# A state-space layer stage: one of four B products moved to GpSimd, six scan tiles, B single-buffered, dt spread one group earlier

## The chip, the cores and the metric

The kernel runs on one core of a Trainium2 chip. The metric is the device time of one launch in microseconds (us), median of several runs; lower is better. The core has five engines with queues of their own: TensorE (PE: matrix products into PSUM), VectorE (DVE), ScalarE (ACT: activations and copies), GpSimd (POOL) and SyncE (SP, here the queue from which most DMAs are issued).

## The reference, cut to what matters

The reference is four blocks in a row on an image of 2 x 128 x 64 x 64; the change touches the first alone. That block runs two layers over a sequence of 4096 positions with 128 channels. A layer is a selective state-space mixer followed by a feed-forward block:

```
t2 = layernorm(t);  xz = t2 @ in_w.T;  u, z = split(xz)
u = silu(causal_conv4(u) + conv_b)                      # 256 channels
dt, Bm, Cm = split(u @ xproj_w.T, [8, 24])              # 8 | 16 | 16
dt = softplus(dt @ dt_w.T + dt_b)                       # 256 channels
dA  = exp(dt[..., None] * A);  dBu = (dt * u)[..., None] * Bm
h   = dA_t * h + dBu_t          # for each of 256 x 16 states, along the sequence
y   = sum_n h[n] * C_t[n] + u * D;  t = t + (y * silu(z)) @ out_w.T
t   = t + gelu(layernorm(t) @ w1.T + b1) @ w2.T + b2
```

The other three blocks (a convolutional attention, a linear-projection attention and a multi-scale fusion) follow; their code is not touched.

## The kernel before, in words

All arithmetic is float32. The first block is written by hand as one long order of instructions (`tc.manual_schedule()`): nothing is reordered, each engine executes its own instructions in the order in which Python emits them, and waits between engines are put in from the tiles that they read and write.

The work is cut into 32 **items** (image b, layer l, chunk c of 512 positions; `items`). The scan of an item needs 256 x 16 states = 4096 rows of 512 positions; with 128 partitions this is 32 scan instructions. They form 8 **groups** g of 4: a group covers 32 channels, partition 32q+d holds channel d with state 4q+m, and m = 0..3 are the four scans of the group. So an item has 32 **slots** t, one scan each, and group g has slots 4g to 4g+3. (In this text the groups of an item are numbered 0 to 7, and the first groups of the next item continue as n0, n1.)

For one group these helpers run, always in this order of data:

- `spread_dt` (L329): four DMAs on SP copy 32 channels of dt to all four partition quarters, tile `dtb` (four buffers). Emitted at the first slot of a group for the group two ahead.
- `decay` (L347, ACT): `da` = exp(A * dtb), one per scan, emitted four slots ahead of its scan, into one of four PSUM buffers. So `da` for slot t+4 needs the buffer of scan t.
- `spread_dtu` (L334, PE): dt*u spread to the quarters by a matrix product, tile `pdu`, one PSUM buffer, emitted one group ahead. It has to wait until the product of the group before has read `pdu`.
- `times_b` (L340, DVE): the **B product** `h` = `bb` * `pdu`, 128 x 2048 (all four m at once), emitted in the last slot of the group before. `bb` holds B of the item, spread to 128 partitions by DMA (two buffers).
- `scan` (L358, DVE): four scans, each 128 x 512, in place in `h`. After the fourth GpSimd saves the last column (L360, `carry`) and multiplies by C (L361, `h` = `h` * `cb`, 128 x 2048).
- `y_pair` (L373, PE): sums over the states of two groups, every second group; `y_out` (L381, DVE) adds u * D when half an item is complete.

`h` tiles come from a ring of five, tag `h`, which also serves the feed-forward's `hid`.

Around this the function `background` emits, slot by slot, the rest of the layer for neighbouring items: for the next item (n) the convolution (slots 0 to 5, L262, L268), silu (slot 11, L282), the x projection (13, 14, L291, L295), softplus of dt (17, L315), dt*u on GpSimd (18, L321); for the item before (p) the second `y_out` and the gate on GpSimd (6, L381, L384), the mixer's output product and its add (8 and 10, L390, L394), the feed-forward's upper half (30, 31, L403); for the one before that (q) gelu and the lower half (3 to 9, L407, L415, L424). Two layer norms share one chain: variance (17, L210 on PE), epsilon and reciprocal root on ACT (18, 19, L214 to L221), and one Newton step: a product on GpSimd, an affine step on ACT, a product on GpSimd (20 and 21, L226, L227, L231), spread on PE and scaled on DVE (27, 28, L235, L239).

The places in the order that matter here, inside one slot: first the spreads, then the scan, then the decay of slot t+4, then (last slot of a group) the B product of the next group, then the background of that slot. B and C are sent through DRAM (`spread_bc`): one store and eight spreading DMAs, 256 KB each, all at slot 14 on SP, ahead of the dt spreads of later groups in the same queue.

```
if m == 0 and 0 <= g + 2 < NG:
    spread_dt(g + 2)
...
if m == 3 and 0 <= g + 1 < NG:
    times_b(g + 1)
for f, a in todo[t_]:
    f(*a)
```

Of the kernel before, what the change touches and what calls it, by code (L numbers as in the profile page):

```python
# [6 lines left out]
F32 = mybir.dt.float32  # L7
AF = mybir.ActivationFunctionType
ALU = mybir.AluOpType
# [6 lines left out]
P = 128  # L16
CH = 512
# [3 lines left out]
DS = 16  # L21
DI = 2 * C
NJ = DI // P
R = (C + 15) // 16
NX = R + 2 * DS
KC = 4
# [41 lines left out]
def tile_conv_seq(ctx: ExitStack, tc, x, consts, vecs, wemb, wlay, wconv, wdt, wqkv, wsmall, wms, out):  # L68
    nc = tc.nc
# [38 lines left out]
    with ExitStack() as s, tc.manual_schedule():  # L108
# [25 lines left out]
        for l in range(NL):  # L134
            w = wp.tile([P, NWL - DI], F32, name=f"wl{l}")
            nc.sync.dma_start(w, wlay[l][:, DI:])
            cw = sp.tile([P, KC + 1, DI], F32, name="cw", tag="h", bufs=5)
            nc.sync.dma_start(cw[:, :KC, :].rearrange("p k d -> p (k d)"), wconv[l : l + 1, :].to_broadcast([P, KC * DI]))
            nc.sync.dma_start(cw[:, KC, :], wlay[l][:, :DI])
            d = wp.tile([R, DI], F32, name=f"wd{l}")  # L140
            nc.sync.dma_start(d, wdt[l])

            u = wp.tile([P, KC, DI], F32, name=f"wu{l}")
            for k in range(KC):
                nc.vector.tensor_tensor(u[:, k, :], cw[:, KC, :], cw[:, k, :], ALU.mult)
            an = wp.tile([P, NJ * DS], F32, name=f"an{l}")
            nc.scalar.activation(an, vec[:, VEC[f"A_log{l}"] : VEC[f"A_log{l}"] + NJ * DS], AF.Exp)
            nc.vector.tensor_scalar(an, an, -1.0, None, ALU.mult)
            a = wp.tile([P, NJ, 4, 4], F32, name=f"am{l}")
            for g in range(4):  # L150
                pa = mm.tile([P, NJ, DS], F32, name="pa", tag="mm")
                nc.tensor.matmul(pa.rearrange("p j n -> p (j n)"), lhsT=four(g), rhs=an, start=True, stop=True)
                for q in range(4):
                    at = slice(32 * q, 32 * q + 32)
                    nc.vector.tensor_copy(a[at, :, g, :], pa[at, :, 4 * q : 4 * q + 4])
            wl.append(w), wu.append(u), wd.append(d), am.append(a)
# [40 lines left out]

        def ln_square(w, k, i):
            if "sq" not in w:
                w["sq"] = sp.tile([P, 2, CH], F32, name="sq", tag="tmp", bufs=2)  # L200
                w["cen"] = sp.tile([P, 2, CH], F32, name="cen", tag="cen")
            pc = w.pop(("pc", k))
            nc.scalar.activation(w["sq"][:, k, :], pc, AF.Square)
            nc.scalar.copy(w["cen"][:, k, :], pc)
# [35 lines left out]

        def ln_shift(w, k, i, second):
            if second:
                dst = st[i]["x2"] = sp.tile([P, CH], F32, name="x2", tag="tmp", bufs=2)
            else:
                xn = st[i]["xn"] = sp.tile([P, KC - 1 + CH], F32, name="xn", tag="xn", bufs=2)
                if items[i][2] == 0:
                    nc.gpsimd.memset(xn[:, : KC - 1], 0.0)
                else:
                    nc.gpsimd.tensor_copy(xn[:, : KC - 1], prev_xn[0][:, CH : CH + KC - 1])
                prev_xn[0] = xn  # L250
                dst = xn[:, KC - 1 :]
            nc.scalar.activation(dst, w["cen"][:, k, :], AF.Identity, bias=vl("ln_b", i))  # L252
# [41 lines left out]
            st[i]["dbl"] = sp.tile([NX, CH], F32, name="dbl", tag="dbl")  # L294
            nc.scalar.copy(st[i]["dbl"], st[i].pop("pd"))  # L295

        def spread_bc(i):

            dr = dp.tile([2 * DS, CH], F32, name="dr", tag="dr")
            nc.sync.dma_start(dr, st[i]["dbl"][R:])  # L300
            for k in range(2):
                o = st[i]["bc", k] = sp.tile([P, 4, CH], F32, name=("bb", "cb")[k], tag=("bb", "cb")[k], bufs=2)
                for q in range(4):
                    src = dr[k * DS + 4 * q : k * DS + 4 * q + 4, :].rearrange("(o m) f -> o (m f)", o=1)
                    nc.sync.dma_start(o[32 * q : 32 * q + 32].rearrange("p m f -> p (m f)"), src.to_broadcast([32, 4 * CH]))

        def dtproj(i, j):
            st[i]["pt", j] = mmt("pt")
# [15 lines left out]
        def spread_dt(g):  # L324
            i, s_ = divmod(g, NST)
            o = st[i]["dtb", s_] = sp.tile([P, CH], F32, name="dtb", tag="dtb", bufs=4)
            k = 32 * (s_ % 4)
            for q in range(4):
                nc.sync.dma_start(o[32 * q : 32 * q + 32, :], st[i]["dt"][k : k + 32, s_ // 4, :])  # L329

        def spread_dtu(g):
            i, s_ = divmod(g, NST)
            pdu = st[i]["pdu", s_] = bc.tile([P, CH], F32, name="pdu", tag="bc")
            nc.tensor.matmul(pdu, lhsT=four(s_ % 4), rhs=st[i]["dtu"][:, s_ // 4, :], start=True, stop=True)  # L334

        def times_b(g):
            i, s_ = divmod(g, NST)
            h = st[i]["h", s_] = sp.tile([P, 4, CH], F32, name="h", tag="h", bufs=5)
            pdu = st[i].pop(("pdu", s_))
            nc.vector.tensor_tensor(h, st[i]["bc", 0], pdu.unsqueeze(1).to_broadcast([P, 4, CH]), ALU.mult)  # L340

        def decay(t):
            g, m = divmod(t, 4)
# [53 lines left out]
        def ffn_up(i, f):  # L397
            w = st[i]
            if f == 0:
                w["hid"] = sp.tile([P, 4, CH], F32, name="hid", tag="h", bufs=5)  # L400
            ph = mmt("ph")
            at = WL_W1 + f * P
            nc.tensor.matmul(ph, lhsT=wl[items[i][1]][:, at : at + P], rhs=w["x2"], start=True, stop=True)  # L403
            nc.scalar.activation(w["hid"][:, f, :], ph, AF.Identity, bias=vl("ffn_b1", i, f))
# [32 lines left out]
        def background(i):  # L437

            todo = [[] for _ in range(NSL)]

            def at(t, f, *a):
                todo[t].append((f, a))

            n, p, q, r = i + 1, i - 1, i - 2, i + 2
            if has(q):
                at(3, gelu, q)
                at(6, ffn_down, q, (0, 1)), at(7, ffn_down, q, (2, 3)), at(9, ffn_add, q)
                at(11, out_mm, q), at(12, out_add, q)
            if has(p):
                at(6, y_out, p, 1), at(6, gate, p)  # L450
                at(8, mix_out, p), at(10, mix_add, p)
            if has(n):
                at(0, pu_taps, n, 0, (0, 1)), at(1, pu_taps, n, 0, (2, 3)), at(2, pu_out, n, 0)
                at(3, pu_taps, n, 1, (0, 1)), at(4, pu_taps, n, 1, (2, 3)), at(5, pu_out, n, 1)
                at(13, xproj, n), at(14, xproj_out, n), at(14, spread_bc, n)
                at(15, dtproj, n, 0), at(16, dtproj, n, 1), at(17, soft_plus, n), at(18, dt_end, n)
            if has(i):
                at(1, pz_mm, i, 0), at(3, pz_out, i, 0)
                at(5, pz_mm, i, 1), at(6, pz_out, i, 1)
            if has(i) or has(n):  # L460
                at(11, silu, i, n)
            pair = [(k, second) for k, second in ((p, True), (r, False)) if has(k)]
            if has(r):
                at(10, embed, r), at(11, embed_out, r)
            w, m = {}, len(pair)
            for k, (it, second) in enumerate(pair):
                at(12 + 2 * k, ln_centre, w, k, it)
                at(13 + 2 * k, ln_square, w, k, it)
                at(27, ln_spread, w, k, m), at(28, ln_scale, w, k, it)
                at(29, ln_shift, w, k, it, second)  # L470
            if pair:
                at(17, ln_var, w, m), at(18, ln_eps, w, m), at(19, ln_rs, w, m), at(20, ln_newton, w, m), at(21, ln_step, w, m)
            if has(p):
                for f in range(4):
                    at(30 + f // 2, ffn_up, p, f)
            if has(i):
                at(23, y_out, i, 0)
            return todo
# [6 lines left out]
        for i in range(-2, NI + 2):  # L485
            todo = background(i)
            for t_ in range(NSL):
                t = i * NSL + t_
                g, m = divmod(t, 4)
                if m == 0 and 0 <= g + 2 < NG:  # L490
                    spread_dt(g + 2)
                if m == 0 and 0 <= g + 1 < NG:
                    spread_dtu(g + 1)
                if m == 0 and g % 2 == 1 and 0 <= g - 3 < NG:
                    y_pair(g - 3)
                if 0 <= t < NT:
                    scan(t)
                if 0 <= t + 4 < NT:
                    decay(t + 4)
                if m == 3 and 0 <= g + 1 < NG:  # L500
                    times_b(g + 1)
                for f, a in todo[t_]:
                    f(*a)


    wbig = ctx.enter_context(tc.tile_pool(name="wbig", bufs=1))
# [11 lines left out]
    with ExitStack() as s, tc.manual_schedule():  # L518
# [10 lines left out]
        st = {}  # L529
# [151 lines left out]
        def at(f, u0):  # L681

            r, u = divmod(now - u0, NU)
            if 0 <= r < len(runs):
                f(r, u)
# [485 lines left out]
```

## Time and profile before

Median 5351.36 us (5349.31 to 5352.06). The profiled execution has a span of 5360.6 us. The stage of the first block runs from the start to about 2170 us of it; its steady part, read as a window from 80 to 2170 us of the span:

| engine | busy us in 2090 us | share | what it mostly does there (mean of one) |
|---|---|---|---|
| DVE | 1882.7 | 90% | 1024 scans (1267 ns), 256 B products (2266 ns) |
| PE | 1835.1 | 88% | state sums, spreads, convolution, projections |
| ACT | 1472.6 | 70% | 1024 decays (685 ns), six table loads an item (1283 ns) |
| POOL | 1430.7 | 68% | 256 C products (4534 ns), dt*u, gate, two norm products an item |

The mean granted TensorE clock in the window is 0.89. How to read what follows: "busy" is the sum of the durations of an engine's instructions; an instruction's "idle before" is the time in which its engine stood still just ahead of it, put down to what ended last. The timeline lists instructions of one engine in order of time, equal ones in a row merged ("x3"), with that idle time in brackets.

### The profile page before, as it was taken

What the parts mean: (1) busy time and instruction counts of PE and PEld (TensorE: products, weight loads), DVE (VectorE), ACT (ScalarE), POOL (GpSimd) and SP (SyncE); (2) the same over time, 40 slices, a digit from 0 to 9 for tenths busy, and PEclk for the clock granted to TensorE, in tenths of its full rate; (3) what the DMA queues carried; (4) which work ended last, traced back from release to release, by engine and by line L of the source; (5) the groups of instructions that cost most, each with busy time, mean ns of one, the idle gap of its engine ahead of it and who ended that gap; (6) DMA issues with size and microseconds to landing.
All of it is one profiled execution on the core that took longest, in us unless ns stands there. A gap on an engine that the chain in (4) does not pass through costs nothing.

```text
span 5360.6 us, 48695 instructions
## 1 busy us (share of the span) xinstructions
PE 4900.6 (91%) x15085; PEld 2311.3 (43%) x15085; DVE 3798.2 (71%) x3810; ACT 2326.4 (43%) x2933; POOL 2287.5 (43%) x1948
## 2 busy tenths in 40 slices
PE   5888888888888898899999999999999998988997
PEld 1222222222222222356665566656666665333332
DVE  4998999889999999136663366667767775656665
ACT  4676777777777776212221122232323221223332
POOL 2766666666666767112221122223333332322221
PEclk8898889999898988899999999999999999999998
DMA  4222233222222232014442244444444442000000
GB/s 108 69 65 64 65 70 70 68 68 64 64 64 64 68 73 69 17 42 95 96 97 50 51 96 96 95 101 112 112 101 101 112 111 71 4 4 4 6 6 8
DMA packets 233843, 362.04 MB, mean 68 GB/s; under 512 B 87648, under 2 KB 88048, under 8 KB 225136
## 3 DMA queue, kind: packets, MB, share of 16 engines
q1 hardware_dynamic: 184432, 291.76, 23.2%
q10 hardware_dynamic: 49152, 67.17, 5.2%
q8 instruction: 121, 1.98, 0.2%
q14 instruction: 138, 1.13, 0.1%
HBM read 83.92 MB, written 6.29 MB: 17 GB/s over the span
## 4 chain that ended last, share of the span: by engine, by line
PE 59%; DVE 14%; DMA 10%; ACT 6%; SPq 4%; issue 4%; POOL 4%; ACTq 0%; DVEq 0%; POOLq 0%
PE pq L600 11%; PE po L647 11%; PE py L373 5%; PE pp L544 5%; DVE tr L627 4%; PE pu L262 4%; SPq L638 3%; DMA dtb<-dt 3%; DVE h L358 3%; DMA bb<-dr 3%; POOL h L361 3%; DMA pt<-tr 3%; PE pdu L334 2%; PE pf L861 2%; PE ph L403 2%
## 5 line engine op out<-in xcount | busy, mean ns | idle before, releaser
L634 POOL COPY pt<-tr 32x512 f32<-32x512 f32 x1024 | 628.0, 613 | 1680.7 <-DVE tr L627 911.8
L358 DVE TENSOR_TENSOR_SCAN h<-da,carry,h 128x512 f32<-128x512 f32 x1024 | 1240.2, 1267 | 97.6 <-ACT da L347 68.3
L361 POOL TENSOR_TENSOR h<-h,cb 128x2048 f32<-128x2048 f32 x256 | 1160.7, 4534 | 20.8 <-POOL carry L360 0.2
L604 DVE TENSOR_SCALAR_CACHE_REDUCE sc<-pq 128x1024 f32<-128x1024 f32 x512 | 625.9, 1223 | 760.6 <-PE pq L600 748.4
L647 PE MATMUL po<-pt,vt 128*128 128x256 f32 x4096 | 968.1, 380 | 4.8 <-DMA pt<-tr 4.8
L600 PE MATMUL pq<-k,q 128*128 128x512 f32 x2048 | 962.1, 592 | 4.8 <-ACT q L532 3.4
L647 PEld LDWEIGHTS po<-pt,vt 128*128 128x128 f32 x4096 | 776.4, 190 | 265.4 <-issue 170.6
L347 ACT ACTIVATE da<-dtb,am 128x512 f32<-128x512 f32 x1024 | 686.8, 685 | 390.3 <-DVE h L358 250.2
L613 ACT ACTIVATE sc<-sc,nm 128x4096 f32<-128x4096 f32 x128 | 474.8, 3709 | 721.9 <-DVE nm L611 615.6
L627 DVE STREAM_TRANSPOSE tr<-sc 128x2048 f32<-128x2048 f32 x256 | 589.3, 2302 | 37.9 <-DMA pt<-tr 24.5
L340 DVE TENSOR_TENSOR h<-bb,pdu 128x2048 f32<-128x2048 f32 x256 | 580.0, 2266 | 25.0 <-POOL carry L360 15.4
L373 PE MATMUL py<-h,sel 128*32 128x512 f32 x2048 | 506.7, 638 | 1.7 <-POOL h L361 1.7
L600 PEld LDWEIGHTS pq<-k,q 128*128 128x128 f32 x2048 | 383.5, 190 | 277.8 <-issue 248.7
L334 PE MATMUL pdu<-dtu,fsel 128*128 128x512 f32 x512 | 327.4, 726 | 87.8 <-DVE h L340 87.6
L532 ACT ACTIVATE q<-pqq,vec 128x256 f32<-128x256 f32 x64 | 30.4, 474 | 606.6 <-PE pqq L544 361.2
L373 PEld LDWEIGHTS py<-h,sel 128*32 128x32 f32 x2048 | 114.5, 117 | 412.5 <-issue 406.8
L544 PE MATMUL pp<-xt,wq 128*128 128x512 f32 x576 | 251.8, 598 | 6.6 <-DMA wq<-in_wqkv 6.2
L262 PE MATMUL pu<-xn,wu 128*128 128x512 f32 x512 | 246.1, 614 | 2.7 <-ACT xn L252 1.7
L235 PE MATMUL pr<-rs,kc 2*128 2x512 f32 (+1 forms) x128 | 117.1, 1059 | 133.1 <-POOL rs L231 126.9
L334 PEld LDWEIGHTS pdu<-dtu,fsel 128*128 128x128 f32 x512 | 95.2, 214 | 303.5 <-DVE h L340 187.9
L888 PE MATMUL pqkv<-f,ws 128*128 128x512 f32 x384 | 197.8, 641 | 10.2 <-ACT q L895 6.3
L950 DVE TENSOR_TENSOR ov<-v,pw 128x2048 f32<-128x2048 f32 x64 | 146.2, 2284 | 63.4 <-PE pw L943 63.3
(191 smaller groups left out, 5089.1 us busy)
## 6 DMA issues: line engine op xcount, KB each, us to landing
pt<-tr SPq DMA_DIRECT2D x2048, 64.0 KB, 2.0
dtb<-dt SPq DMA_DIRECT2D x1024, 64.0 KB, 2.0
pt<-tr ACTq DMA_DIRECT2D x1024, 64.0 KB, 2.1
bb<-dr SPq DMA_DIRECT2D x128, 256.0 KB, 4.5
cb<-dr SPq DMA_DIRECT2D x128, 256.0 KB, 7.6
xt<-in_x SPq DMA_DIRECT2D x16, 256.0 KB, 5.1
xr<-in_x SPq DMA_DIRECT2D x16, 256.0 KB, 3.1
out<-ot SPq DMA_DIRECT2D x16, 256.0 KB, 2.0
```

What stands on the lines that cost most here:

```text
L334: nc.tensor.matmul(pdu, lhsT=four(s_ % 4), rhs=st[i]["dtu"][:, s_ // 4, :], start=True, stop=True)
L340: nc.vector.tensor_tensor(h, st[i]["bc", 0], pdu.unsqueeze(1).to_broadcast([P, 4, CH]), ALU.mult)
L347: nc.scalar.activation(da, st[i]["dtb", s_], AF.Exp, scale=am[items[i][1]][:, j, gg, m : m + 1])
L358: nc.vector.tensor_tensor_scan(h[:, m, :], da, h[:, m, :], carries[b, l][:, j, gg, m : m + 1], ALU.mult, ALU.add)
L361: nc.gpsimd.tensor_tensor(h, h, st[i]["bc", 1], ALU.mult)
L373: nc.tensor.matmul(py[r : r + 32, :], lhsT=sel, rhs=st[i]["h", s_ + k][:, m, :], start=(m == 0), stop=(m == 3), tile_position=(0, r),)
L544: nc.tensor.matmul(ps, lhsT=wq[:, which, tap, :], rhs=rhs, start=(tap == 0), stop=(tap == 8))
L600: nc.tensor.matmul(pq[:, i, :], lhsT=st["q", r, grp][:, it * P : (it + 1) * P], rhs=st["k"][:, at : at + CH], start=True, stop=True)
L604: nc.vector.tensor_scalar(dst, pq, 1.0, None, ALU.mult, ALU.max, accum_out=st["mx"][:, c2 : c2 + 1])
L627: nc.vector.transpose(tr, half.rearrange("p (t r f) -> p r t f", r=NB, f=32))
L634: nc.gpsimd.tensor_copy(dst, src)
L647: nc.tensor.matmul(st["po", r, grp], lhsT=st["vt"][:, jt, :], rhs=rhs, start=(jt == 0), stop=(jt == N // P - 1))
```

## The change

Five edits, all in the first block:

1. The B product of a group is split. VectorE multiplies m = 0, 1, 2 (128 x 1536) and GpSimd m = 3 (128 x 512, `times_b_last`). [...]ScalarE first copies `pdu` from PSUM to a new tile `dub` (`copy_dtu`, one buffer). The copy is emitted in the second slot of the group before, right after the decay; GpSimd's product in the third slot, after the background of that slot. This is to relieve VectorE.
2. The ring of `h` tiles grows from five to six, since GpSimd's product takes its tile one slot earlier.
3. B has one buffer in place of two, which pays for the sixth `h` tile in memory. The store (`store_bc`) stays at slot 14; C is spread at slot 16, and B at slot 27, when the last B product of the running item has been emitted.
4. dt is spread three groups ahead in place of two.
5. `sq` and `x2` of the norms no longer share a two-buffer tag (memory only).

```
-                st[i]["bc", k] ... tag=("bb", "cb")[k], bufs=2      # all at slot 14
+        def store_bc(i): ...                                      # slot 14
+        def spread_bc(i, k):
+            o = ... tag="bc"[k] + "b", bufs=1 + k                 # C slot 16, B slot 27
...
+        def copy_dtu(g):
+            i, s_ = divmod(g, NST)
+            o = st[i]["dub", s_] = sp.tile([P, CH], F32, name="dub", tag="dub")
+            nc.scalar.copy(o, st[i]["pdu", s_])
+
+        def times_b_last(g):
+            i, s_ = divmod(g, NST)
+            h = st[i]["h", s_] = sp.tile([P, 4, CH], F32, name="h", tag="h", bufs=6)
+            nc.gpsimd.tensor_tensor(h[:, 3, :], st[i]["bc", 0][:, 3, :], st[i].pop(("dub", s_)), ALU.mult)
+
         def times_b(g):
             i, s_ = divmod(g, NST)
-            h = st[i]["h", s_] = sp.tile([P, 4, CH], F32, name="h", tag="h", bufs=5)
+            h = st[i]["h", s_]
             pdu = st[i].pop(("pdu", s_))
-            nc.vector.tensor_tensor(h, st[i]["bc", 0], pdu.unsqueeze(1).to_broadcast([P, 4, CH]), ALU.mult)
+            nc.vector.tensor_tensor(h[:, :3, :], st[i]["bc", 0][:, :3, :], pdu.unsqueeze(1).to_broadcast([P, 3, CH]), ALU.mult)
...
-                at(13, xproj, n), at(14, xproj_out, n), at(14, spread_bc, n)
+                at(13, xproj, n), at(14, xproj_out, n), at(14, store_bc, n), at(16, spread_bc, n, 1), at(27, spread_bc, n, 0)
...
-                if m == 0 and 0 <= g + 2 < NG:
-                    spread_dt(g + 2)
+                if m == 0 and 0 <= g + 3 < NG:
+                    spread_dt(g + 3)
...
                     decay(t + 4)
+                if m == 1 and 0 <= g + 1 < NG:
+                    copy_dtu(g + 1)
                 if m == 3 and 0 <= g + 1 < NG:
                     times_b(g + 1)
                 for f, a in todo[t_]:
                     f(*a)
+                if m == 2 and 0 <= g + 1 < NG:
+                    times_b_last(g + 1)
```

More of the change, by code (lines that the diff above doesn't have):

```diff
@@ L136, in tile_conv_seq @@
             nc.sync.dma_start(w, wlay[l][:, DI:])
-            cw = sp.tile([P, KC + 1, DI], F32, name="cw", tag="h", bufs=5)
+            cw = sp.tile([P, KC + 1, DI], F32, name="cw", tag="h", bufs=6)
             nc.sync.dma_start(cw[:, :KC, :].rearrange("p k d -> p (k d)"), wconv[l : l + 1, :].to_broadcast([P, KC * DI]))
@@ L199, in ln_square @@
             if "sq" not in w:
-                w["sq"] = sp.tile([P, 2, CH], F32, name="sq", tag="tmp", bufs=2)
+                w["sq"] = sp.tile([P, 2, CH], F32, name="sq", tag="sq")
                 w["cen"] = sp.tile([P, 2, CH], F32, name="cen", tag="cen")
@@ L242, in ln_shift @@
             if second:
-                dst = st[i]["x2"] = sp.tile([P, CH], F32, name="x2", tag="tmp", bufs=2)
+                dst = st[i]["x2"] = sp.tile([P, CH], F32, name="x2", tag="x2")
             else:
@@ L295, in xproj_out, with store_bc @@
             nc.scalar.copy(st[i]["dbl"], st[i].pop("pd"))
[L297 to L305, printed above, removed]
+        def store_bc(i):
+            st[i]["dr"] = dp.tile([2 * DS, CH], F32, name="dr", tag="dr")
+            nc.sync.dma_start(st[i]["dr"], st[i]["dbl"][R:])
+        def spread_bc(i, k):
+            o = st[i]["bc", k] = sp.tile([P, 4, CH], F32, name="bc"[k] + "b", tag="bc"[k] + "b", bufs=1 + k)
+            for q in range(4):
+                src = st[i]["dr"][k * DS + 4 * q : k * DS + 4 * q + 4, :].rearrange("(o m) f -> o (m f)", o=1)
+                nc.sync.dma_start(o[32 * q : 32 * q + 32].rearrange("p m f -> p (m f)"), src.to_broadcast([32, 4 * CH]))
         def dtproj(i, j):
@@ L399, in ffn_up @@
             if f == 0:
-                w["hid"] = sp.tile([P, 4, CH], F32, name="hid", tag="h", bufs=5)
+                w["hid"] = sp.tile([P, 4, CH], F32, name="hid", tag="h", bufs=6)
             ph = mmt("ph")
```

## The prediction, made before the changed kernel ran

> **What bounds the kernel now.** I read the busy shares of the first block's steady part (80 to 2170 us), then the groups by line, then, since shares average over a repeating pattern, the timeline of one item engine by engine. The window (columns: PE, PEld, DVE, ACT, POOL busy, granted clock, DMA share, GB/s) and VectorE's two big groups:
>
> ```profile
> 80.00:2170.00 2090.00, 1835.12 (x4618) 558.93 (x4617) 1882.68 (x1405) 1472.60 (x2082) 1430.66 (x671) 0.89 0.29 67
> ...
> L358 DVE TENSOR_TENSOR_SCAN h<-da,carry,h 128x512 f32<-128x512 f32 x1024 | 1240.2, 1267 | 97.6 <-ACT da L347 68.3 <-POOL carry L356 5.7
> L340 DVE TENSOR_TENSOR h<-bb,pdu 128x2048 f32<-128x2048 f32 x256 | 580.0, 2266 | 25.0 <-POOL carry L360 15.4 <-issue 5.3 <-PE pdu L334 3.0
> L381 DVE SCALAR_TENSOR_TENSOR u<-u,vec,py 128x512 f32<-128x512 f32 x64 | 47.8, 747 | 84.9 <-PE py L373 84.9
> ```
>
> VectorE is the fullest engine (90%), but TensorE has 88%, and VectorE stands still for known reasons: 84.9 us for TensorE's state sums ahead of `y_out`, 68.3 us for decays. So one item next, VectorE first. The item's cycle is taken from the end of the last B product of the item before (916.85 + 2.26 = 919.1) to that of its own (981.44 + 2.26 = 983.7): 64.6 us.
>
> ```profile
> 940.64 0.75 DVE L381 SCALAR_TENSOR_TENSOR u<-u,vec,py 128x512 f32<-128x512 f32 x1 [1.79 <-PE py L373]
> ...
> 971.36 2.26 DVE L340 TENSOR_TENSOR h<-bb,pdu 128x2048 f32<-128x2048 f32 x1
> 974.10 0.75 DVE L381 SCALAR_TENSOR_TENSOR u<-u,vec,py 128x512 f32<-128x512 f32 x1 [0.48 <-PE py L373]
> 976.68 4.85 DVE L358 TENSOR_TENSOR_SCAN h<-da,carry,h 128x512 f32<-128x512 f32 x4 [1.83 <-ACT da L347]
> 981.44 2.26 DVE L340 TENSOR_TENSOR h<-bb,pdu 128x2048 f32<-128x2048 f32 x1
> ```
>
> The reader is to see three stops an item (1.79, 0.48, 1.83), and that the B product of group 6 runs at 971.36. ScalarE in the same item:
>
> ```profile
> 951.29 0.59 ACT L394 COPY xt<-po 128x512 f32<-128x512 f32 x1 [2.05 <-PE po L391]
> ...
> 963.85 1.28 ACT L315 ACT_TABLE_LOAD   x1
> 965.15 1.27 ACT L315 ACTIVATE dt<-pt,vec 128x512 f32<-128x512 f32 x2
> ...
> 971.38 0.63 ACT L221 ACTIVATE nt<-rs 2x512 f32<-2x512 f32 x1
> 975.95 0.69 ACT L347 ACTIVATE da<-dtb,am 128x512 f32<-128x512 f32 x1 [3.94 <-DMA dtb<-dt]
> 976.58 0.71 ACT L227 ACTIVATE nt<-nt,c 2x512 f32<-2x512 f32 x1
> ```
>
> From 951.29 (after TensorE's `po`) to 968 ScalarE has no gap: it is late, not loaded evenly. At 971.38 it is done with the norm's root and then stands 3.94 us for dt's DMA, queued on SP behind B and C. GpSimd:
>
> ```profile
> 966.49 2.34 POOL L321 TENSOR_TENSOR dtu<-dt,u 128x1024 f32<-128x1024 f32 x1 [4.85 <-ACT dt L315]
> 968.78 0.19 POOL L360 COPY carry<-h 128x4 f32<-128x4 f32 x1
> 969.04 4.55 POOL L361 TENSOR_TENSOR h<-h,cb 128x2048 f32<-128x2048 f32 x1
> 973.56 1.26 POOL L226 TENSOR_TENSOR nt<-nt,ve 2x512 f32<-2x512 f32 x1
> 977.36 1.25 POOL L231 TENSOR_TENSOR rs<-rs,nt 2x512 f32<-2x512 f32 x1 [2.54 <-ACT nt L227]
> ```
>
> dt*u waits for softplus, the C product of group 4 stands behind it, and the Newton product behind that. ScalarE's L227 needs the Newton product; today it comes (974.82) before dt's DMA has landed (975.9), so it costs nothing. TensorE's timeline shows no gap from 919 to the matrix product at 963.46: 951.29 is set by TensorE, 32.2 us after the cycle's start, whatever VectorE does.
>
> **What the Trainium skill says.** "TensorE: Matmul & The Clock Gate" (Architectural detail) has ACT, DVE and GpSimd as strict first-in-first-out queues; the trace agrees: behind the decay that waited 3.94 us nothing of ScalarE ran. "PSUM — Partial Sum Buffer" (PSUM bank collisions raise a hardware error) says that two engines reading one bank at once collide, so reads by ScalarE and VectorE of one bank must be ordered. The kernel before has no second reader of `pdu`; the changed program does, and in it every B product on VectorE waits for exactly the `copy_dtu` of its group. "SBUF — State Buffer" (Who interferes with whom) says that a VectorE instruction with at most one SBUF input does not contend with GpSimd. Product (`bb`, `pdu`) and scan (`da`, `h`) have one each besides a small carry; the trace agrees, the C product is 4.51 to 4.55 us beside any of them. So more GpSimd work slows nobody by itself. "TensorE: Matmul & The Clock Gate" (What's actually happening) says that an idle window of about 3.4 us halves TensorE's clock; here the spread products take 2.08 us at 983.76 after idle and 1.02 us at 947.66.
>
> **The change part by part.**
>
> *VectorE's product gets shorter.* 2048 columns take 2.26 us. With a fixed part of 0 to 0.4 us, 1536 take 1.70 to 1.79; I take 1.73, so 0.53 us a group, 256 x 0.53 = 136 us over the stage, if VectorE set the pace. It does not everywhere. Between 919.1 and 940.6 it would only wait longer for `py` (two products, 1.06 us, added to the 1.79).
>
> *GpSimd's quarter.* A product of 512 columns takes 1.26 us (L226), from the C product's rate 1.13; I take 1.26. 8 an item are 10 us on 45 busy of 65: it fits, but its place matters. It is in front of `carry` and the C product in GpSimd's queue.
>
> *ScalarE's copy.* 128x512 from PSUM, 0.59 us (L394). Where ScalarE has gaps it is hidden. Of slots 1, 5, 9 the row of gaps ahead of 951.29 absorbs all. Slots 13 and 17 lie in the gapless stretch: softplus ends 2 x 0.58 = 1.15 us later, 967.6 for 966.4.
>
> *dt three ahead, C and B moved.* dt of the groups concerned is issued before or well clear of C, so the 3.94 us wait goes. B in one buffer: its four DMAs start when group 7's product has read `bb`; issues are about 0.4 apart and land in 4.5 us (2.9 to 6.2), so 6 to 7.5 us after 919.1. VectorE wants it after 6.2 us; up to 1.3 us of waiting, hidden in the longer wait for `py`. I put it at zero. *Six tiles* remove the small waits ahead of group 0's product (15.4 us in all), in the same hidden stretch: zero.
>
> *The new wait.* In ScalarE's order behind softplus stand: decays 22 and 23 and the root, decay 24, L227, decay 25, then the copy for group 6. VectorE's group 6 product must wait for that copy, and the scans of group 6 are queued behind it. Followed through:
>
> - dt*u from 967.6: 967.6 + 2.35 = 970.0; GpSimd's quarter of group 5, + 1.26 = 971.2; carry, + 0.2; C product of group 4, + 4.55 = 975.95; Newton product, + 1.26 = 977.2.
> - ScalarE, decay 24 long done: L227 0.75 = 977.95; decay 25 0.63 = 978.6; copy 0.6 = 979.2.
> - VectorE: group 6's product 979.2 + 1.75 = 980.95 (before, it began at 971.36); `y_out` 0.7 and switch 0.1; to group 7's product four scans, 981.44 - 976.68 = 4.76; product 1.75; end 988.15 for 983.7.
>
> That is 4.45 us more an item. The next cycle starts from there with the same 32.2 us of TensorE. Softplus and dt*u occur 31 times: 31 x 4.45 = 138 us; 5351 + 138 = **5489 us**.
>
> **Rivals.**
>
> *A, VectorE stays the bound and all else is hidden:* 136 us and the 68.3 us for decays go: 5147. For it: 90% busy. Against: the `py` waits, and ScalarE's position behind VectorE. 5%.
>
> *B, the copy's wait is hidden at group 6:* if ScalarE passed its copy by 973, `y_out` would still wait for `py`, whose chain (variance after softplus) moves by 1.15: 974.10 + 1.15 = 975.25, then 0.7, 4.76, 1.75: 982.45, 1.25 less an item, 39 us: 5312. Against it stands the fixed order of the queues. 12%.
>
> *C, TensorE cools further:* it will stand idle longer ahead of group 7's spread and the next cycle (now 3.58 and 2.80). Two more windows of 3.4 us at half clock cost 3.4 us an item, 105 us: 5594, with less for one window. 10%.
>
> *D, the forecast's size:* 4.45 an item could be 2.9 to 6 by the bounds above (copy 0.48 to 0.69 by three, quarter 1.13 to 1.26, B late by 1.3 if not hidden): 5441 to 5537. 70%. No change at all: 3%.
>
> So slower 80%, same 3%, faster 17%. The range takes in D and most of C: 5425 to 5585.
>
> **What would show it.** Right: VectorE's product about 1.73 us; ahead of it in group 6 an idle of several us put down to ScalarE's copy; ScalarE's L227 waiting for GpSimd; no dt wait; VectorE's busy share falling towards 80%; stage cycle near 69 us. Wrong: group 6's product starting near 973, or ScalarE's L227 without a wait, or the quarter well over 1.3 us, or a `py` wait that does not grow.

## The result, and the profile after

The changed kernel takes 5494.69 us (5489.81 to 5496.95) against 5351.23 us before: ratio 1.0266, 95% interval 1.0251 to 1.0282. It is 143 us slower; 138 us slower was forecast.

VectorE's groups of the first block in the changed kernel, in the window 80 to 2310 us (the stage is that much longer; columns as before: busy, mean ns, idle before and what ended it):

```profile
L370 DVE TENSOR_TENSOR_SCAN h<-da,carry,h 128x512 f32<-128x512 f32 x1024 | 1240.4, 1266 | 35.1 <-ACT da L359 13.3 <-POOL carry L368 13.2 <-POOL h L346 0.4
L352 DVE TENSOR_TENSOR h<-bb,pdu 128x1536 f32<-128x1536 f32 x256 | 445.7, 1741 | 336.2 <-ACT dub L341 304.2 <-DMA bb<-dr 21.7 <-ACT da L359 9.9
L393 DVE SCALAR_TENSOR_TENSOR u<-u,vec,py 128x512 f32<-128x512 f32 x64 | 47.6, 744 | 103.6 <-PE py L385 103.6
```

The B product lost 134 us of work (580.0 to 445.7) and gained 311 us of idle (25.0 to 336.2), of which 304.2 are waits for ScalarE's copy `dub`. The scans wait 62 us less. VectorE's share of the window is 1752.7 of 2230 us, 79%: VectorE has less work, but the time grew.

One item of the changed kernel, VectorE (timeline, idle time in brackets):

```profile
991.87 0.75 DVE L393 SCALAR_TENSOR_TENSOR u<-u,vec,py 128x512 f32<-128x512 f32 x1 [2.80 <-PE py L385]
...
1010.78 1.75 DVE L352 TENSOR_TENSOR h<-bb,pdu 128x1536 f32<-128x1536 f32 x1 [3.54 <-ACT dub L341]
...
1030.35 1.75 DVE L352 TENSOR_TENSOR h<-bb,pdu 128x1536 f32<-128x1536 f32 x1 [6.04 <-ACT dub L341]
1032.03 0.74 DVE L393 SCALAR_TENSOR_TENSOR u<-u,vec,py 128x512 f32<-128x512 f32 x1
1032.68 4.80 DVE L370 TENSOR_TENSOR_SCAN h<-da,carry,h 128x512 f32<-128x512 f32 x4
1037.40 1.73 DVE L352 TENSOR_TENSOR h<-bb,pdu 128x1536 f32<-128x1536 f32 x1
```

and, in the same item, the chain that ends in that copy, GpSimd first and then ScalarE:

```profile
1018.92 2.35 POOL L322 TENSOR_TENSOR dtu<-dt,u 128x1024 f32<-128x1024 f32 x1 [2.07 <-ACT dt L316]
1021.22 1.30 POOL L346 TENSOR_TENSOR h<-bb,dub 128x512 f32<-128x512 f32 x1
1022.47 0.18 POOL L372 COPY carry<-h 128x4 f32<-128x4 f32 x1
1022.73 4.53 POOL L373 TENSOR_TENSOR h<-h,cb 128x2048 f32<-128x2048 f32 x1
1027.23 1.25 POOL L226 TENSOR_TENSOR nt<-nt,ve 2x512 f32<-2x512 f32 x1
```

```profile
1024.71 0.67 ACT L359 ACTIVATE da<-dtb,am 128x512 f32<-128x512 f32 x1
1028.51 0.72 ACT L227 ACTIVATE nt<-nt,c 2x512 f32<-2x512 f32 x1 [3.13 <-POOL nt L226]
1029.14 0.67 ACT L359 ACTIVATE da<-dtb,am 128x512 f32<-128x512 f32 x1
1029.75 0.57 ACT L341 COPY dub<-pdu 128x512 f32<-128x512 f32 x1
```

The reader is to follow one line to the next: dt*u, the new quarter and the C product stand one behind the other on GpSimd without a gap; the Newton product ends at 1028.48, ScalarE's L227 starts at 1028.51, the copy ends at 1030.32 and VectorE's product starts at 1030.35. dt's DMA is no longer in the chain: decay 24 (1024.71) follows without a wait where it waited 3.94 us before. This cycle, from the end of one group 7 product (968.62 + 1.73 = 970.35) to the end of the next (1039.13), takes 68.8 us; the item shown of the kernel before took 64.6. As means over 29 items it is 69.75 us for 65.27.

### The profile page after: what moved, and what is told of

Same layout as the page of the kernel before. It is cut to its first block, busy times and chain, and to the rows that moved or that the text cites. A ratio compares the mean times of both kernels' runs of the same rounds, so it can differ in the third digit from the quotient of the medians.

```text
span 5490.4 us, 49041 instructions
## 1 busy us (share of the span) xinstructions
PE 4946.3 (90%) x15085; PEld 2321.1 (42%) x15085; DVE 3667.8 (67%) x3810; ACT 2459.0 (45%) x3189; POOL 2603.3 (47%) x2204
## 3 DMA queue, kind: packets, MB, share of 16 engines
q14 instruction: 140, 1.15, 0.1%
## 4 chain that ended last, share of the span: by engine, by line
PE 60%; DVE 16%; ACT 8%; POOL 6%; issue 3%; SPq 3%; DMA 3%; ACTq 0%; DVEq 0%; POOLq 0%
PE pq L616 12%; PE po L663 12%; PE pp L560 5%; PE py L385 5%; DVE h L370 4%; PE pu L262 4%; DVE tr L643 4%; DVE h L352 3%; POOL h L373 3%; SPq L654 3%; PE pdu L335 3%; PE pf L877 2%; DMA pt<-tr 2%; PE pf L427 2%; PE ph L415 2%
## 5 line engine op out<-in xcount | busy, mean ns | idle before, releaser
L352 DVE TENSOR_TENSOR h<-bb,pdu 128x1536 f32<-128x1536 f32 x256 | 445.7, 1741 | 336.2 <-ACT dub L341 304.2
L335 PE MATMUL pdu<-dtu,fsel 128*128 128x512 f32 x512 | 350.4, 773 | 238.9 <-DVE h L352 238.9
L346 POOL TENSOR_TENSOR h<-bb,dub 128x512 f32<-128x512 f32 x256 | 331.6, 1296 | 252.9 <-ACT dub L341 130.4
L970 POOL TENSOR_TENSOR ov<-ov 128x2048 f32<-128x2048 f32 x16 | 72.6, 4539 | 251.3 <-DVE ov L966 251.3
```

Of the source, the lines that this page charges most:

```text
L352: nc.vector.tensor_tensor(h[:, :3, :], st[i]["bc", 0][:, :3, :], pdu.unsqueeze(1).to_broadcast([P, 3, CH]), ALU.mult)
```

## The experiments

All are measured against the kernel before in the same session, whose median there lay between 5355 and 5358 us. Per-item waits below are means over 29 items of the trace. A place "of the item" is counted from the item's first scan, which starts a little over 9 us after the cycle's start as it is taken above.

**1. The copy one slot earlier.**

```
-                if m == 1 and 0 <= g + 1 < NG:
+                if m == 0 and 0 <= g + 1 < NG:
                     copy_dtu(g + 1)
```

> The changed kernel with the ScalarE copy emitted one slot earlier (first slot of a group, ahead of the Newton step in slot 20). Theory (the copy for group 6 stands in ScalarE's queue behind the Newton step, which waits for GpSimd): the copy of group 6 is done some 4 us earlier, VectorE's wait at group 6 falls from 5.96 us to about 1 to 2, an item to about 65 us, the time to about 5360 (31 x 4.3 us less than 5495). Rival, GpSimd's quarter itself delays C products and state sums: 5480 to 5500. Rival, B in one buffer: 5480 to 5500. Rival, the copies' own time on ScalarE: 5480 to 5500.

Measured: 5428.45 us, ratio 1.0129 (1.0114 to 1.0144). The wait ahead of group 6's product fell from 5.96 to 1.60 us, as forecast, and half of the loss went: 71 us are left of 143. Much of the other half stayed because a second wait came up, ahead of group 0, 3.73 us an item in place of 0.88 (experiment 5 says how much). VectorE, GpSimd and the DMA queue of that kernel at that place:

```profile
1009.02 1.73 DVE L352 TENSOR_TENSOR h<-bb,pdu 128x1536 f32<-128x1536 f32 x1
...
1020.75 1.75 DVE L352 TENSOR_TENSOR h<-bb,pdu 128x1536 f32<-128x1536 f32 x1 [3.84 <-DMA bb<-dr]
```

```profile
1012.13 1.29 POOL L346 TENSOR_TENSOR h<-bb,dub 128x512 f32<-128x512 f32 x1
```

```profile
1013.45 1.70 SPq L306 DMA_DIRECT2D bb<-dr  x4
```

VectorE has read B for the last time at 1010.75, but GpSimd's quarter of group 7, behind a C product, reads it until 1013.42; only then do B's DMAs start (1013.45), and VectorE's next product, which needs them, starts 7.3 us later. In the changed kernel the quarter of group 7 is done 1.3 us before VectorE's product ends (means over 29 items), so B's DMAs start at 1039.19, right behind that product (1039.13), and 0.88 us of waiting is left. The rival "B in one buffer" is thus not the cause of the loss, but it is the next bound.

**2. Copy and quarter left off.** VectorE makes the whole product; all else of the change stays.

```
-                if m == 1 and 0 <= g + 1 < NG:
-                    copy_dtu(g + 1)
...
-            nc.vector.tensor_tensor(h[:, :3, :], ... to_broadcast([P, 3, CH]), ALU.mult)
+            nc.vector.tensor_tensor(h, st[i]["bc", 0], pdu.unsqueeze(1).to_broadcast([P, 4, CH]), ALU.mult)
...
-                if m == 2 and 0 <= g + 1 < NG:
-                    times_b_last(g + 1)
```

> The changed kernel with VectorE making the whole B product again, without copy and without GpSimd's quarter; six tiles, B in one buffer, C and B at slots 16 and 27 and dt three groups ahead stay. Theory: all the loss comes with copy and quarter, and dt's wait is gone for good, so the scans of group 6 start about 1.9 us earlier than in the kernel before: about 5351 - 31 x 1.9 = 5293. Rival, B in one buffer costs: over 5400. Rival, dt's DMA was hidden by the Newton step anyway: 5340 to 5355.

Measured: 5337.92 us, ratio 0.9962 (0.9948 to 0.9977), 20 us faster than before where 58 were expected. So the loss does come with copy and quarter, and the rest of the change is a small gain. The expected gain was too large by 1.2 us an item. About half of that goes with the wait ahead of `y_out` of the first half, 0.66 us an item: `y_out` starts at 46.93 of the item (46.02 before), because TensorE's variance products, which stand ahead of the state sums, got slower. The group in the kernel before and here (400 to 2000 us; columns busy, mean ns):

```profile
L210 PE MATMUL var<-sq,kc 128*2 128x512 f32 x96 | 63.1, 793 | 34.1 <-ACT dt L315 34.1
```

```profile
L210 PE MATMUL var<-sq,kc 128*2 128x512 f32 x100 | 83.9, 990 | 35.4 <-ACT dt L316 35.4
```

The four products of an item start at nearly the same place (38.15 of the item, 37.91 before), yet end 0.9 us later (41.42 for 40.50). The trace's clock record goes with it: from 37 to 43 of the item TensorE is granted 0.60 of its clock as a mean over 29 items, 0.75 before, and the median of one product is 1057 ns for 634. Most of the other part goes with the last scan of group 5. It waits 0.61 us an item (0.18 before) for its decay, which stands in ScalarE's queue behind the norm's epsilon step, and that step waits for the same variance products, 0.82 us an item (0.29 before). ScalarE's wait for GpSimd's Newton product, 63.1 us in all, holds VectorE for only 0.12 us an item here.

**3. The copy kept, but not used.** As experiment 2, with `copy_dtu` left where the change put it; VectorE makes the whole product and nobody reads `dub`.

> The changed kernel with the copy kept but not used: VectorE makes the whole B product, GpSimd none. Theory (the copy and the wait of VectorE for it are the cost): softplus stays 1.15 us late, the Newton product comes 1.3 us earlier than in the changed kernel, VectorE's product is 0.53 us longer in two groups on the path: about 69 us an item, 5470 to 5490, nearly as slow as the changed kernel although GpSimd has no more work than before. Rival, GpSimd's quarter in its queue is the cost: about 5310 to 5350.

Measured: 5512.35 us, ratio 1.0287 (1.0272 to 1.0303). With no new work on GpSimd at all, the kernel is as slow as the changed one. VectorE's product here:

```profile
L352 DVE TENSOR_TENSOR h<-bb,pdu 128x2048 f32<-128x2048 f32 x256 | 581.6, 2272 | 269.8 <-ACT dub L341 235.1 <-DMA bb<-dr 22.3 <-ACT da L359 11.9
```

It waits 235.1 us for a copy whose data no one uses: VectorE and ScalarE read the same PSUM tile, and the program puts their reads in order. So the copy alone is enough for the loss, and the rival "GpSimd's quarter is the cost" falls. The time is 22 us above the forecast of 5470 to 5490. ScalarE needs 16.8 us from the copy of `po` to the end of softplus, 16.2 in the changed kernel: in between, its decays now wait 0.52 us an item for VectorE's scans. That is about 19 us over 31 items.

**4. The changed kernel without the Newton step.** Both GpSimd products and ScalarE's affine step are left out.

```
-  at(19, ln_rs, w, m), at(20, ln_newton, w, m), at(21, ln_step, w, m)
+  at(19, ln_rs, w, m),
```

> The changed kernel without the Newton step of the layer norms (both GpSimd products and ScalarE's affine step are left out, so the reciprocal root is less refined); the copy stays where it was. Theory (ScalarE's wait for GpSimd inside the Newton step is what holds the copy of group 6): ScalarE reaches that copy at about 47 us of the item in place of 50.8, an item is 3.7 us shorter, about 5380. Rival, the copies' own time on ScalarE or GpSimd's quarter: 5470 to 5495 (only the 2.5 us an item of GpSimd time go, off the path).

Measured: 5370.68 us, ratio 1.0020 (1.0014 to 1.0027). The kernel is 13 us slower than before in place of 143, although every copy, quarter and buffer is as in the changed kernel. VectorE's product here:

```profile
L352 DVE TENSOR_TENSOR h<-bb,pdu 128x1536 f32<-128x1536 f32 x255 | 444.1, 1741 | 219.6 <-ACT dub L341 183.8 <-DMA bb<-dr 21.0 <-ACT da L359 8.2
```

The wait at group 6 is 2.20 us for 5.96. That shows where the copy was held: behind the Newton step in ScalarE's queue. Of the 3.8 us by which the wait fell, 3.1 were ScalarE's wait for GpSimd's product in the changed kernel (mean over 29 items) and 0.7 the affine step itself; GpSimd's second product was not ahead of the copy.

**5. The early copy, group 7 whole on VectorE.** Experiment 1, with copy and quarter emitted only where `(g + 1) % NST < NST - 1`, and `times_b` over all four m in group 7.

> The kernel with the early copy (5428), and group 7's B product whole on VectorE again, so that GpSimd's late quarter no longer holds the one B buffer. Theory (the 3.73 us wait ahead of group 0 is B's DMA, issued only after GpSimd's quarter of group 7 at 58.0 of the item, 2.6 us after VectorE's part): that wait falls to about 1.2 us; part of it comes back as a longer wait for the state sums (1.9 becomes about 3) and 0.53 us of VectorE, so about 0.9 us an item or 27 us less, 5400. Rival, the wait is the DMA's own length: the wait stays above 3 us and the time at 5428 to 5445.

Measured: 5388.22 us, ratio 1.0056 (1.0042 to 1.0070), 40 us less than experiment 1 (27 forecast). The wait ahead of group 0 is 1.00 us, that for the state sums at `y_out` rose from 1.92 to 2.97. So most of the 3.73 us came from GpSimd's late read of B, not from the DMA's length. 31 us more than before are left; group 4 still waits 2.59 us an item for its copy and group 6 1.60, and what each of these costs was not separated.

**6. The quarter for group 7 alone.** Experiment 2, with copy and quarter put back only where `(g + 1) % NST == NST - 1`.

> The kernel without copy and quarter (5338), with both put back for group 7 alone, where ScalarE has gaps. Theory (the split pays where ScalarE is in step and VectorE sets the pace): 0.53 us an item, 17 us, about 5321. Rival, any split costs: 5338 or more, up to 5360 if GpSimd's quarter holds B's buffer for longer than the wait for the state sums hides.

Measured: 5322.72 us, ratio 0.9936 (0.9924 to 0.9949), 15 us less than experiment 2, and 12 us less than experiment 7, which ran in the same session. That is a small step: the runs of this kernel lie between 5319.76 and 5331.02. At group 7, where ScalarE is in step, the split gives about what it takes off VectorE.

**7. dt two groups ahead.** Experiment 2, with `spread_dt(g + 2)` as before.

> The kernel without copy and quarter (5338), with dt spread two groups ahead as before; C and B stay at slots 16 and 27. Theory A (dt's wait went because C and B no longer stand ahead of dt in the queue): 5335 to 5345, no dt wait of over 0.5 us an item. Theory B (it went because dt starts a group earlier): the wait of about 4 us comes back, 5350 to 5365.

Measured: 5335.11 us, ratio 0.9957 (0.9943 to 0.9970); no wait for dt of that kind comes back: ScalarE's decays wait for it three times, 9.3 us in all, in place of 31 times and 133.9 us. SP's queue in the kernel before (950 to 985 us) and here (940 to 1010 us) shows what differs:

```profile
962.74 1.69 SPq L305 DMA_DIRECT2D bb<-dr  x4
964.53 1.76 SPq L305 DMA_DIRECT2D cb<-dr  x4
966.34 19.06 SPq L329 DMA_DIRECT2D dtb<-dt  x24
```

```profile
949.87 2.41 SPq L330 DMA_DIRECT2D dtb<-dt  x4
952.39 1.92 SPq L306 DMA_DIRECT2D cb<-dr  x4
954.36 5.52 SPq L330 DMA_DIRECT2D dtb<-dt  x8
971.13 1.70 SPq L306 DMA_DIRECT2D bb<-dr  x4
```

The four transfers of dt for group 6 now go out ahead of C and B. So dt's wait went because C and B no longer stand ahead of it in SP's queue; the third group ahead does nothing measurable.

**8. Two waits moved behind work that is ready.** Experiment 2, with ScalarE's affine step (and GpSimd's second product, which needs it) at slot 22 and the item's first `y_out` at slot 25.

```
-  at(20, ln_newton, w, m), at(21, ln_step, w, m)
+  at(20, ln_newton, w, m), at(22, ln_affine, w, m), at(22, ln_step, w, m)
...
-                at(23, y_out, i, 0)
+                at(25, y_out, i, 0)
```

(`ln_newton` keeps the product on GpSimd; `ln_affine` holds the line of ScalarE.)

> The kernel without copy and quarter (5338), with two waits moved behind work that is ready: ScalarE's affine step of the Newton refinement at slot 22 in place of 20, and the first y_out of an item at slot 25 in place of 23. Theory (after the copy is gone these two hold the scans of groups 5 and 6): VectorE's waits of 0.65 us for the state sums and 0.6 us for decays go, 1.2 us an item, about 5301. Rival, TensorE's stretch from the cycle's start sets the item whatever VectorE does later: 5330 to 5340.

Measured: 5304.44 us, ratio 0.9901 (0.9886 to 0.9916): the best kernel here, 1% faster than before. The cycle is 63.27 us as a mean, 64.52 in experiment 2: the 1.2 us an item came, but not from the two places named. The wait for the state sums went (0.66 us an item to none). The wait of group 5's last scan for its decay only fell from 0.61 to 0.45, since it hangs on the variance products, not on the affine step. The rest lies at the start of the item, where the first `y_out` of the cycle comes 0.4 us earlier; what moved it was not tried. Both steps were moved at once, so their shares were not separated.

**9. Experiments 6 and 8 together.**

> Both gains together: copy and quarter for group 7 alone, affine step at slot 22, first y_out at slot 25. Theory (the two act in different places of the item): up to 16 us less than the 5304 of the second, about 5290, somewhat less gained if B's DMA, held by GpSimd's quarter of group 7, takes the place of the waits that went. Rival, the later Newton steps push that quarter so far back that B comes after TensorE's stretch: 5310 or more.

Measured: 5311.82 us, ratio 0.9921 (0.9908 to 0.9935). The gains do not add; whether the two together are slower than experiment 8 alone is not clear, since the intervals of the two ratios overlap. VectorE's product with its waits for B's DMA, experiment 8 and then this kernel (80 to 2150 us):

```profile
L355 DVE TENSOR_TENSOR h<-bb,pdu 128x2048 f32<-128x2048 f32 x256 | 579.7, 2264 | 35.4 <-DMA bb<-dr 26.7 <-PE pdu L338 3.3 <-DMA dtb<-dt 2.0
```

```profile
L358 DVE TENSOR_TENSOR h<-bb,pdu 128x2048 f32<-128x2048 f32 (+1 forms) x256 | 562.5, 2197 | 94.4 <-DMA bb<-dr 69.4 <-PE ph L421 15.9 <-DMA dtb<-dt 6.4
```

As its rival had it, GpSimd's quarter of group 7 holds the one B buffer. It ends 1.88 us after VectorE's own product of group 7 (1.15 in experiment 6), B's DMAs start right behind it, and group 0's product of the next item starts at 8.97 us of the cycle in place of 7.14 in experiment 8 (means over 29 items).

## Why the prediction was right

*TensorE's stretch.* It was forecast to stay at 32.2 us. In the item shown the copy of `po` starts at 1002.54, 32.19 us after 970.35; over 29 items the median is 32.73 us, 32.75 before. Two things were wrong with it. "Whatever VectorE does" is too strong: in experiment 1, where group 0's product comes late, the mean is 34.84. And the mean in the changed kernel is 0.37 us higher than before (33.25 for 32.88), mostly from the three items that begin a new layer or a new image. There the first scan waits until GpSimd has cleared `carry`, and GpSimd, with its new products, comes to that later. Before and after:

```profile
604.54 4.81 DVE L358 TENSOR_TENSOR_SCAN h<-da,carry,h 128x512 f32<-128x512 f32 x4 [1.91 <-POOL carry L356]
```

```profile
635.34 4.81 DVE L370 TENSOR_TENSOR_SCAN h<-da,carry,h 128x512 f32<-128x512 f32 x4 [4.41 <-POOL carry L368]
```

This is 13.2 us in all for 5.7 (5.4 in experiment 3, which has no quarter), and the prediction did not have it.

*VectorE waits longer ahead of the first `y_out`.* Forecast 1.06 us more; measured as a mean over 29 items 3.07 for 2.02, 1.05 more. The prediction put B's late arrival at group 0 at zero because that longer wait would hide it, and the stretch's unchanged median agrees: the wait ahead of group 0 is 0.88 us, 0.68 before.

*Softplus 1.15 us late.* From the copy of `po` to the end of softplus: 1018.85 - 1002.54 = 16.31 us for 966.42 - 951.29 = 15.13, 1.18 more.

*The chain through GpSimd and ScalarE.* From the end of softplus to the start of group 6's product 11.6 us were worked out (967.6 to 979.2); measured 1030.35 - 1018.85 = 11.5, and 11.51 as a mean. Experiments 3, 4 and 1 show its links one by one: the order of the two reads, ScalarE's wait in the Newton step, the copy's place behind it.

*The sizes.* VectorE's product 1741 ns (1.73 forecast), GpSimd's quarter 1296 ns (1.26), copy 0.57 to 0.59 us. 143 / 31 = 4.6 us an item for 4.45; in the two traces the mean cycle grew by 4.48. That it is so close is in part luck: the stretch, put at no change, gave 0.37 us, and the part behind softplus grew by 2.93 us, not by the 3.25 that the working has (988.15 - 967.6 for 983.7 - 966.4). The two misses nearly cancel.

*What was left out.* The wait at group 4 (3.46 us an item) was not named. It costs little on its own: ScalarE sets the same softplus, and on its way from the copy of `po` to there it waits for VectorE's scans only 0.03 us an item.

*Slips in the working.* The last sum names a switch of 0.1 us and leaves it out: 980.95 + 0.7 + 0.1 + 4.76 + 1.75 is 988.26, which makes 4.56 us an item and 5492. The low end of D, 2.9 us an item, does not come from the bounds named there; they take off about 0.45 and leave 4.0, or 5475. Neither changes the forecast.

*What was right only in this kernel.* One B buffer at no cost: true while group 6 is late, a bound of its own as soon as it is not (experiments 1, 5, 9).

*The rivals.* A falls with the 304.2 us of waits for `dub`, B with the start of group 6's product, 6.04 us of idle behind the copy. C did not come as a cost: the mean granted clock of the stage fell from 0.89 to 0.86, but the median of TensorE's stretch did not move.

## What to carry to other kernels

Here the work moved off the fullest engine was worth nothing where that engine already waited for others. Read the pattern's timeline, find the engine that sets each stretch, and count only the stretches that the engine itself sets (here group 7, experiment 6: 15 us of the 134 us of work). A helper instruction on a third engine couples the two to that engine's queue; look at what stands ahead of the helper in it, and what that waits for. A copy out of a PSUM tile that a second engine reads as well was such a coupling even when nobody used its result (experiment 3, 235.1 us). A second PSUM tile for the copy to read, which VectorE does not touch, was not tried.

## What the runs showed that had not been expected

TensorE's variance products, in the same place of the item and behind the same neighbours, take 990 ns in place of 793 in experiment 2, where the mean granted clock from 37 to 43 of the item is 0.60 in place of 0.75. They end 0.9 us later, and two waits of VectorE grow with them: 0.66 us an item for the state sums (0.48 before) and 0.61 for a decay behind the epsilon step (0.18). No forecast had it. What changed the clock there was not tried.
